# A two-layer decoder on one core: kinds of TensorE products in the plan, a planned expert stage, the last routing group in parts, and one PSUM bank for sums and output

## The chip, the cores and the metric

The kernel runs on one core of a Trainium2 chip. The metric is the device time of one execution in microseconds; lower is better. Engines are named as in the profile: PE (TensorE matmul), PEld (its weight loads), DVE (VectorE), ACT (ScalarE), POOL (GpSimd) and SP (SyncE, whose queue issues most transfers).

## The reference

The input is x of 16 sequences by 256 tokens by 256 features, in float32, with a context of 77 tokens per sequence. Six steps follow one another, each of the form x = x + f(layernorm(x)):

```python
x = x + _L0_attn_ref(_layernorm(x), ...)    # causal linear attention, 16 heads of 16
x = x + _L0_xattn_ref(_layernorm(x), ctx, mask, ...)  # softmax cross attention, 16 heads of 16
x = x + _L0_ffn_ref(_layernorm(x), gate_w, w1, w2)    # 16 experts, top 2, capacity 640 rows
x = x + _L1_attn_ref(_layernorm(x), ...)    # softmax attention, 8 heads of 64, low-rank keys and values
x = x + _L1_xattn_ref(_layernorm(x), ctx, ctx, ..., mask)  # one head of 256
x = x + _L1_ffn_ref(_layernorm(x), ...)     # gated FFN, weights and activations rounded to grids
```

In the expert step every token picks its two best experts by a sigmoid of gate products. A token's row number in its expert's batch is its rank, counted over all tokens in order; ranks of 640 and more are dropped:

```python
logits = xf @ gate_w.T; probs = sigmoid(logits); top_vals, sel = top_k(probs, 2)
weights = top_vals / (top_vals.sum(-1) + 1e-6)
ranks = cumsum(onehot(sel))[sel] - 1; valid = ranks < 640
padded[sel * 640 + ranks] = xf            # scatter
h = gelu(padded @ w1[e]); y = h @ w2[e]   # per expert
out = sum over the two of weights * y[slot]   # gather
```

So no expert can start before the last token has been routed.

## The kernel before, in words

The 4096 tokens are 32 tiles of 128 (NT = 32), four tiles to a group (NG = 8); x stays in SBUF. All products are in float32. The stages follow one another: `l0_attention`, `l0_cross` (which also routes tokens and ends with `latent_weights` and `cross_weights`, products that merge layer 1's weight matrices), `l0_experts`, `l1_tokens` (gathers the experts' rows, then both attentions of layer 1) and `l1_ffn`.

**The plan.** Three of the stages (`l0_attention`, `l0_cross`, `l1_tokens`) record their operations in a `Plan` and issue them afterwards in an order worked out from estimated times. A recorded operation is a `Call`, or several TensorE calls under `together()` which use separate parts of the array side by side. In `Plan.issue` every engine looks at the operations whose inputs are ready, finds the earliest possible begin, and takes the lowest rank among those that can begin within `near` = 150 ns of it. The rank is the place in program order, moved by `urgent`. Before, TensorE pays 100 ns in the plan when it passes from a single product to a group or back:

```python
parts = len(op.calls) > 1
busy += 100 if parts != split else 0
```

A transfer on SP is planned as 60 ns of issue and 2500 ns to landing. `Ring` keeps count of a pool's buffers: a tile can start when the tile that had its buffer before is done, and tiles with one tag start in the order in which they were made. Everything planned shows line L322 in the profile, so instructions are told apart by the tiles they write and read.

**Normalisation.** `layernorm` and `layernorm_act` take statistics on DVE (`bn_stats`, `bn_aggr`), add 1e-5 on DVE (`ln_var`, `la_var`: 128 x 4 values for four tiles), raise to the power -0.5 on POOL (`ln_rstd`, `la_rstd`), and scale on DVE or ACT (`h`, `rh`).

**Cross attention.** For each tile `scores(i)` makes products in two row halves of the array (`ps_sc`), adds the mask (`lx_s`, DVE), takes maxima (`lx_mx`, DVE), subtracts (POOL), exponentiates (ACT) and sums (`lx_sum`, DVE). `weighted(i)` transposes the weights (`ps_pt`, copied to `lx_sT`), spreads and transposes the reciprocals of the sums (`ps_rec`, copied to `rT`), multiplies by the values in column parts (`ps_av`), scales (`lx_aT`), multiplies by the output matrix into the free half of `ps_rec`, and adds to x. The eight PSUM banks are: two for the ring `pp`, four for `ps_sc`, two for the ring `pm` in which `ps_rec` and `ps_av` alternate. `l0_attention` has the same layout and a similar `weighted(i)`.

**Routing.** `R.take(g)` is a generator whose steps are mixed into the tiles of the next group: normalisation (`rh`), transposes (`ps_rt`, `rhT`), gate products (`ps_logit`), the two best experts (`rt_top`, `rt_sel`), counts (`rt_hits`, `rt_cum` on POOL), ranks by products with a triangular matrix (`ps_rank`), row numbers (`slot`), and then eight indirect transfers from POOL's queue, which scatter the rows to `moe_x` in DRAM. The last group is routed after the last tile:

```python
        step(route, 8)
        step(R.take(NG - 1), 8)
```

**Experts.** `l0_experts` is not planned; the compiler's scheduler orders it. For each of the 16 experts SP loads `w1`, `w2` (the tile `w`, 512 KB each) and the 640 rows `ex_xg`, whose load waits for every scatter; PE transposes the rows (`ps_xT`), multiplies by w1 (`ps_h`, Gelu on ACT) and by w2 (`ps_y`), DVE copies to `ex_y`, and SP stores the 640 rows to `moe_y`. Between experts, `ffn_weights` rounds the three weight matrices of the last FFN to their grid (`fw_w`, `fw_s` on DVE) and transposes them (`ps_wT`): 12 transposes for each matrix.

## Time and profile before

| | us |
|---|---|
| median of three runs | 1785.4 |
| lowest and highest of them | 1784.87, 1789.61 |
| the profiled execution, its time | 1783.88 |
| the profiled execution, its span (first to last instruction) | 1782.1 |
| busy in the span: PE, DVE, ACT, POOL | 1634.5, 1131.0, 697.9, 502.9 |
| last x of `l0_attention` | 278.5 |
| last x of `l0_cross` (tile 31) | 609.9 |
| first `ps_h` of the experts | 661.8 |
| last store of the experts issued | 966.4 |

The profile shows one execution. A group row of it reads: line, engine, operation, tile written and tiles read, shape, count, then busy time, mean duration of one in ns, and the idle time of the engine just before these instructions with what ended it. A timeline row reads: start, duration, engine, line, operation, tiles, count, and in brackets idle time before it with its releaser. Matmuls are pipelined and their ends are modelled, so the distance from one start to the next says more of PE than the duration. A float32 product appears as two matmul records.

### The profile page before, as it was taken

To read this page: it belongs to the slowest core of one execution; us is meant where nothing else is said; L and a number is where in the kernel's file an instruction comes from. 1 tells how busy PE (TensorE), PEld (TensorE's weight loads), DVE (VectorE), ACT (ScalarE), POOL (GpSimd) and SP (SyncE) were. 2 spreads that over 40 slices of the span, in tenths; PEclk is the share of its full clock that TensorE was granted. 3 is DMA by queue.
4 is the path that set the end of the run, shared out by engine and by line. 5 is a ranking of instruction groups with operands and counts; after the bars stand their busy time and mean duration, and the time that the engine had idled before them with its cause. 6 is when DMAs were issued, how large, how long until landed. Compare 5 with 4: busy or idle time off the path is not lost.

```text
span 1782.1 us, 24580 instructions
## 1 busy us (share of the span) xinstructions
PE 1634.5 (92%) x9428; PEld 1077.5 (60%) x9428; DVE 1131.0 (63%) x2290; ACT 697.9 (39%) x1467; POOL 502.9 (28%) x547
## 2 busy tenths in 40 slices
PE   5999997999999769999997799999999599989899
PEld 3666664666666557777776466666666344434388
DVE  7867667998888633221212789876767543998751
ACT  2223222655555311111111455465556233656650
POOL 6333213455556420000001776534334100000000
PEclk9999998999999769999999899999999699999999
DMA  5000007210111133343341111000000000000011
GB/s 174 1 1 1 1 1 241 66 32 28 34 34 37 57 131 118 108 147 119 107 133 50 51 57 36 28 1 1 1 1 1 1 0 0 1 0 0 0 45 50
DMA packets 73375, 84.48 MB, mean 47 GB/s; under 512 B 11614, under 2 KB 64566, under 8 KB 73258
## 3 DMA queue, kind: packets, MB, share of 16 engines
q1 hardware_dynamic: 67114, 66.35, 11.7%
q0 software_dynamic: 6144, 16.57, 2.9%
q8 instruction: 74, 1.21, 0.3%
q14 instruction: 43, 0.35, 0.1%
HBM read 49.56 MB, written 33.56 MB: 47 GB/s over the span
## 4 chain that ended last, share of the span: by engine, by line
PE 66%; DVE 21%; issue 7%; ACT 3%; POOL 2%; DMA 1%; SPq 0%; POOLq 0%; DVEq 0%; ACTq 0%
PE ps_h L422 8%; PE ps_y L422 8%; PE ps_pr L322 7%; PE ps_av L322 7%; PE ps_sc L322 6%; PE ps_gate L422 5%; PE ps_out L422 5%; PE ps_pt L322 4%; PE ps_v L322 3%; PE ps_rec L322 3%; PE ps_po L322 3%; DVE x L322 2%; DVE ff_g L1794 2%; DVE ff_ps L1681 2%; PE ps_ht L322 1%
## 5 line engine op out<-in xcount | busy, mean ns | idle before, releaser
L1558 DVE COPY ex_y<-ps_y 128x256 f32<-128x256 f32 x80 | 34.0, 424 | 231.3 <-PE ps_y L422 231.3
L422 PE MATMUL ps_up<-ff_x,ffn_up 128*128 128x512 f32 x384 | 167.6, 595 | 10.6 <-DVE ff_pu L1681 7.8
L322 POOL DMA_INDIRECT ex_yg<-moe_y,slot x64 | 63.2, 988 | 341.6 <-DMA moe_y<-ex_y 321.2
L322 POOL TENSOR_TENSOR sa_e<-sa_e,sa_rec 128x1024 f32<-128x1024 f32 x64 | 121.4, 1904 | 118.0 <-PE ps_pt L322 62.7
L322 ACT ACTIVATE sa_e<-ps_sc,sa_top 128x256 f32<-128x256 f32 x256 | 118.4, 485 | 69.1 <-DVE sa_top L322 65.0
L422 PE MATMUL ps_h<-ex_xT,w 128*128 128x320 f32 x512 | 142.8, 437 | 0.0
L422 PE MATMUL ps_y<-w,ex_h 128*128 128x256 f32 x640 | 140.7, 379 | 0.0
L422 PEld LDWEIGHTS ps_up<-ff_x,ffn_up 128*128 128x128 f32 x384 | 72.1, 190 | 105.9 <-issue 83.0
L422 PEld LDWEIGHTS ps_y<-w,ex_h 128*128 128x128 f32 x640 | 121.6, 190 | 18.2
L1548 ACT ACTIVATE ex_h<-ps_h 128x640 f32<-128x640 f32 x64 | 45.1, 704 | 221.3 <-PE ps_h L422 221.3
L422 PEld LDWEIGHTS ps_h<-ex_xT,w 128*128 128x128 f32 x512 | 96.7, 191 | 40.0 <-issue 0.6
L322 POOL TENSOR_TENSOR lx_s<-lx_s,lx_mx 128x616 f32<-128x616 f32 x64 | 77.5, 1224 | 51.6 <-DVE lx_mx L322 35.1
L422 PE MATMUL ps_out<-ffn_down,ff_g 128*128 128x256 f32 x384 | 85.3, 386 | 7.3 <-issue 7.3
L422 PE MATMUL ps_gate<-ff_x,ffn_gate 128*128 128x512 f32 x192 | 85.4, 608 | 6.4 <-DVE ff_x L1773 6.4
L422 PEld LDWEIGHTS ps_out<-ffn_down,ff_g 128*128 128x128 f32 x384 | 74.4, 194 | 18.7 <-issue 8.1
L322 ACT COPY lx_sT<-ps_pt 77x512 f32<-77x512 f32 x117 | 65.4, 581 | 49.8 <-PE ps_pt L322 49.4
L322 DVE TENSOR_TENSOR la_at<-ps_sc,la_tri 128x1024 f32<-128x1024 f32 x64 | 76.0, 1217 | 13.9 <-PE ps_sc L322 13.9
L322 PE MATMUL ps_pt<-ident,lx_s 128*77 128x128 f32 x512 | 77.0, 285 | 6.4 <-DVE rt_hits L322 3.7
L322 DVE TENSOR_REDUCE sa_top<-ps_sc 128x4 f32<-128x1024 f32 x64 | 75.9, 1214 | 10.7 <-PE ps_sc L322 10.7
L322 PE MATMUL ps_ht<-ident,h 128*128 128x128 f32 x256 | 38.8, 293 | 42.1 <-DVE h L322 24.8
L322 PEld LDWEIGHTS ps_pt<-ident,lx_s 128*77 128x77 f32 x512 | 58.7, 150 | 25.4 <-issue 10.7
L322 POOL DMA_INDIRECT moe_x<-rh,slot x64 | 63.5, 992 | 27.7 <-issue 10.1
(295 smaller groups left out, 3419.4 us busy)
## 6 DMA issues: line engine op xcount, KB each, us to landing
w<-in_L_ffn_w SPq DMA_DIRECT2D x32, 512.0 KB, 4.4
moe_x<-rt_zero SPq DMA_DIRECT2D x16, 640.0 KB, 7.6
ex_xg<-moe_x SPq DMA_DIRECT2D x16, 640.0 KB, 6.9
moe_y<-ex_y SPq DMA_DIRECT2D x16, 640.0 KB, 5.9
x<-in_x SPq DMA_DIRECT2D x32, 128.0 KB, 3.2
out_x<-x SPq DMA_DIRECT2D x32, 128.0 KB, 1.7
w_ctx_T<-in_ctx_T SPq DMA_DIRECT2D x1, 1232.0 KB
lx_bias<-in_mask_Bx1xSxS_ff SPq DMA_DIRECT2D x8, 154.0 KB, 2.4
```

The costliest lines, as they stand in the source:

```text
L322: made = getattr(getattr(self.nc, self.engine), self.method)(*self.args, **self.kwargs)
L422: E.nc.tensor.matmul(ps, a, b, start=n == 0, stop=n == last)
L1548: nc.scalar.activation(h[:, f, :].rearrange("p (a c) -> p a c", a=2), ps[:, :, :HC], AF.Gelu)
L1558: nc.vector.tensor_copy(y[:, c, :], ps)
L1681: E.nc.vector.tensor_reduce(out, in_, axis, ALU.max, apply_absolute_value=True)
L1794: nc.vector.scalar_tensor_tensor(gp, low16(gq, I16), sg16, low16(sig, U16), ALU.mult, ALU.mult)
```

## The change

Six things change.

1. `Plan` knows three kinds of TensorE operation: "all" (a single product), "row" (a `together` group whose parts use up to 64 rows and all columns) and "col" (the other groups). A table `CHANGE` gives the ns between two operations by their kinds; it enters the begin time when TensorE's next operation is chosen. The busy time of a group adds its parts by kind.
2. The normalisations' add of 1e-5 is done on POOL, just before the power, with a constant tile `E.eps`.
3. In both attentions of layer 0, the reciprocals, the sums and the output product of a tile share one bank, `ps_rec`; the sums stand in its first half, and the copy `rT` is made after the sums. In `l0_cross` ring `pp` gets three banks and `pm` one, and the sums of both halves of the heads are one `together` group; in `l1_tokens` both halves of the keys are one group.
4. `R.take` takes a first tile and a number of tiles. The last group is routed in three parts: tiles 28 and 29, tile 30, tile 31, each begun when its last tile has been computed. A scatter's rank is moved back by `later` = 300 operations, for the last two parts by 0. The steps of the last part come after the last tile.
5. `l0_experts` is planned, with rings for its pools. The first expert's rows are loaded in five pieces of 128 rows; the last expert's rows are stored in five.
6. `ffn_weights` records into the same plan, with a PSUM bank of its own.

```diff
+    CHANGE = {
+        ("all", "all"): 0, ("all", "row"): 95, ("all", "col"): 95,
+        ("row", "all"): 205, ("row", "row"): 107, ("row", "col"): 205,
+        ("col", "all"): 120, ("col", "row"): 115, ("col", "col"): 25,
+    }
...
                     begin = max(start, free[call.engine])
+                    if call.engine == "tensor":
+                        begin = max(start, free["tensor"] + self.CHANGE[last, op.first])
...
-                parts = len(op.calls) > 1
-                busy += 100 if parts != split else 0
-                split = parts
+                last = op.last
...
-        parts = {}
+        time, kind, parts = 0, op.first, {}
         for c in op.calls:
+            if c.kind != kind:
+                time += max(parts.values()) + self.CHANGE[kind, c.kind]
+                kind, parts = c.kind, {}
             parts[c.part] = parts.get(c.part, 0) + c.busy
-        return max(parts.values())
+        return time + max(parts.values())
...
+            if together:
+                self.kind = "row" if left.ap[0][1] <= 64 and out.ap[0][1] == P else "col"
...
-    var = pool.tile([P, 4], F32, name="ln_var", tag="ln_var")
-    nc.vector.tensor_scalar(var[:, :n], mv[:, :n, 1], 1e-5, None, ALU.add)
     rstd = pool.tile([P, 4], F32, name="ln_rstd", tag="ln_rstd")
-    nc.gpsimd.tensor_tensor(rstd[:, :n], var[:, :n], E.neghalf[:, :n], ALU.pow)
+    nc.gpsimd.tensor_tensor(rstd[:, :n], mv[:, :n, 1], E.eps[:, :n], ALU.add)
+    nc.gpsimd.tensor_tensor(rstd[:, :n], rstd[:, :n], E.neghalf[:, :n], ALU.pow)
...
-    def take(g):
+    def take(i0, n=4, later=300):
...
             for k in range(2):
-                nc.gpsimd.indirect_dma_start(
+                with nc.urgent(-later):
+                    nc.gpsimd.indirect_dma_start(
...
-        pp = nc.ring(ctx.enter_context(tc.tile_pool(name="lx_pp", bufs=2, space=PSUM)), 2)
+        pp = nc.ring(ctx.enter_context(tc.tile_pool(name="lx_pp", bufs=3, space=PSUM)), 3)
...
-        pm = nc.ring(ctx.enter_context(tc.tile_pool(name="lx_pm", bufs=2, space=PSUM)), 2)
+        pm = nc.ring(ctx.enter_context(tc.tile_pool(name="lx_pm", bufs=1, space=PSUM)), 1)
...
-                    pr[:, m * P : (m + 1) * P],
+                    pr[:, D + m * P : D + (m + 1) * P],
...
-            rT = w3.tile([P, D], F32, name="lx_rT", tag="lx_rT", bufs=2)
-            nc.copy(rT, pr[:, :D])
-            av = pm.tile([P, 512], F32, name="ps_av", tag="pm")
-            for m in range(KD):
-                with nc.together():
+            with nc.together():
+                for m in range(KD):
                     for par in range(2):
                         for j in range(4):
                             nc.tensor.matmul(
-                                av[32 * j : 32 * j + 32, m * P : (m + 1) * P],
+                                pr[32 * j : 32 * j + 32, m * P : (m + 1) * P],
...
+            rT = w3.tile([P, D], F32, name="lx_rT", tag="lx_rT", bufs=2)
+            nc.copy(rT, pr[:, D:])
             aT = w3.tile([P, D], F32, name="lx_aT", tag="lx_aT", bufs=2)
-            nc.vector.tensor_tensor(aT, av[:, :D], rT, ALU.mult)
+            nc.vector.tensor_tensor(aT, pr[:, :D], rT, ALU.mult)
...
-                route = R.take(g - 1) if g else none
+                route = R.take(4 * g - 4) if g else none
...
-            step(route)
+            step(route, 1 if g < NG - 1 else 3)
...
             step(mine)
-        step(route, 8)
-        step(R.take(NG - 1), 8)
+            if g == NG - 1 and a:
+
+                with nc.urgent(-80):
+                    step(route, 8)
+                    step(last, 8)
+                    last = R.take(i - 1, 2) if a == 1 else R.take(i, 1, 0)
+                    step(last, 3)
+        step(last, 8)
...
-    with ExitStack() as ctx:
-        wk = ctx.enter_context(tc.tile_pool(name="ex_w", bufs=2))
...
+    with ExitStack() as ctx, planned(E) as nc:
+        wm = nc.ring(ctx.enter_context(tc.tile_pool(name="ex_m", bufs=2)), 2)
+        wk = nc.ring(ctx.enter_context(tc.tile_pool(name="ex_w", bufs=2)), 2)
...
+            for c in range(0, CT, CT if e else 1):
+                cs = slice(c, c + (CT if e else 1))
+                nc.sync.dma_start(xg[:, cs, :], rows[:, cs, :], then=behind_scatters)
...
-            between(e)
+            rows = routed.yd[batch, :].rearrange("(c p) d -> p c d", p=P)
+            n = 1 if e == NE - 1 else CT
+            for c in range(0, CT, n):
+                nc.sync.dma_start(rows[:, c : c + n, :], y[:, c : c + n, :])
+            between(e, pw)
...
     def make(name, psum, tag):
+        nc = E.nc
+        wk = made.setdefault("ring", nc.ring(pool, 2)) if not made else made["ring"]
```

## The prediction

> **What bounds the kernel now.** I read the busy times by stage first, then the chain of waits, then the timeline where the chain is not TensorE. The first view has columns for length, busy time (instructions) of PE, PE's weight loads, DVE, ACT and POOL, granted clock, DMA share and GB/s.
>
> ```profile
> core 0: us, PE busy (x) PEld busy (x) DVE busy (x) ACT busy (x) POOL busy (x), PEclk, DMA share, GB/s
> 46.00:275.00 229.00, 225.00 (x2170) 151.41 (x2172) 158.53 (x291) 64.32 (x140) 64.48 (x92) 1.00 0.01 1
> 307.00:552.00 245.00, 223.80 (x1886) 149.46 (x1887) 219.84 (x532) 131.77 (x250) 128.43 (x153) 0.95 0.14 45
> 552.00:610.00 58.00, 51.46 (x463) 36.49 (x461) 44.79 (x124) 26.93 (x50) 31.59 (x41) 0.88 0.09 30
> 610.00:662.00 52.00, 30.15 (x127) 23.66 (x128) 22.54 (x56) 8.24 (x16) 14.00 (x16) 0.59 0.35 120
> 662.00:966.50 304.50, 303.11 (x1316) 235.73 (x1314) 66.77 (x165) 47.59 (x69) 0.00 (x0) 1.00 0.35 114
> 1000.00:1417.00 417.00, 395.61 (x2202) 258.66 (x2198) 315.97 (x671) 220.71 (x745) 198.11 (x145) 0.97 0.05 15
> ```
>
> Rows 1, 5 and 6 (first attention, experts, layer 1) have PE busy 98%, 99.5% and 95%: there only less PE work helps. Row 2 (cross attention with routing) has PE at 91% and DVE at 90%, neither full. In row 4 the kernel is between two stages: 52 us, PE busy 30 of it, at 0.59 of its clock. So the places to gain in are rows 2 to 4. A group row and the timeline say what slows row 2:
>
> ```profile
> L322 DVE TENSOR_SCALAR la_var<-la_mv 128x4 f32<-128x4 f32 x7 | 14.9, 2132 | 0.2
> 577.69 2.46 DVE L322 TENSOR_SCALAR la_var<-la_mv 128x4 f32<-128x4 f32 x1
> 577.70 2.41 POOL L322 TENSOR_TENSOR lx_s<-lx_s,lx_mx 128x616 f32<-128x616 f32 x2
> 580.23 1.04 POOL L322 TENSOR_TENSOR la_rstd<-la_var,neghalf 128x4 f32<-128x4 f32 x1
> 580.53 1.13 PE L322 MATMUL ps_rec<-w_L_xattn_wo,lx_aT 128*128 128x256 f32 x4 [2.69 <-DVE lx_aT L322]
> ```
>
> A DVE instruction on 4 columns takes 2132 ns on average, and in the example 2.46 us, exactly as long as the two POOL subtractions beside it (577.70, 2.41 us for two); at 610.57, with POOL on a scatter, it took 0.17. DVE held behind POOL makes lx_aT late, and PE idles 2.69 us. The chain of waits has this instruction at 2.63, 1.82, 2.60, 2.57, 2.58 and 2.47 us, at 376.68 to 577.69, once per group of four tiles. Now the hand-over between cross attention and experts:
>
> ```profile
> 609.44 0.42 DVE L322 TENSOR_TENSOR x<-x,ps_rec 128x256 f32<-128x256 f32 x1 [1.22 <-PE ps_rec L322]
> 617.13 3.60 PE L322 MATMUL ps_logit<-w_L_ffn_gate_wT,rhT 128*128 128x16 f32 x16 [0.46 <-ACT rhT L322]
> 623.95 1.74 DVE L1663 TENSOR_TENSOR fw_w<-fw_w,fw_r 128x1536 f32<-128x1536 f32 x1
> 631.48 0.66 PE L322 MATMUL ps_rank<-rt_hits,rt_before 128*128 128x64 f32 x2 [10.75 <-DVE rt_both L322]
> 646.30 0.97 POOL L322 DMA_INDIRECT moe_x<-rh,slot  x1 [0.31 <-DMA moe_x<-rh,slot]
> 648.29 0.42 DVE L322 TENSOR_TENSOR cx_vb<-ps_bv,r_L_xattn_bo 77x256 f32<-77x256 f32 x1 [1.07 <-PE ps_bv L322]
> 648.77 0.37 SPq L1519 DMA_DIRECT2D w<-in_L_ffn_w  x1
> 659.02 1.51 PE L1538 MATMUL ps_xT<-ident,ex_xg 128*128 128x128 f32 x6
> 661.82 9.75 PE L422 MATMUL ps_h<-ex_xT,w 128*128 128x320 f32 x32
> ```
>
> Tile 31 is finished at 609.86. Its group is routed only then: 16 gate products for four tiles, DVE work on FFN weights (fw_w, L1663) between the small routing instructions, PE idle 10.75 us before the ranks, the products that merge layer 1's weights (631.93 to 648.29), cx_vb, and only behind cx_vb the first expert's weights on SP (the waits of SP's queue give L1519 38.3 us behind cx_vb). 52.0 us pass from tile 31 to the first ps_h.
>
> **The change part by part.** The profiled execution took 1783.9 us (span 1782.1 and 1.8 around it); the median shown is 1785.4, 1.5 more. I sum against 1783.9.
>
> *A. The normalisation's add moves from DVE to POOL.* la_var goes: six instances on the chain are 14.7 us together, and I take -14.7. ln_var goes too (40 at 276 ns, 11.0 us over the kernel), mostly where PE is the bound, so 0. POOL gets about 50 adds; the nearest row is rt_cum, 288 ns, so 14.5 us on an engine busy 28%. The add stands before the power on POOL (1.04 us) with scatters and subtractions queued behind: 0.1 us net in a handover, since a wait DVE to POOL goes. Bounds: 0 if the next DVE instruction gets stuck in the same way, -17.5 (all seven at about 2.5).
> The Trainium skill bears on this ("SBUF — State Buffer", section "SBUF: two separate sides"): DVE and POOL share a port pair, an exclusive lock which the one that starts first holds for its whole instruction. By the rule la_var would get in after one subtraction (1.2 us), and seven would be worth 8.4; the row has it waiting for two. I take the row. The rule also speaks against the change: an instruction with two SBUF inputs, such as the routing's wgt, can be caught in la_var's place, and the new POOL add takes the same pair.
>
> *B. The rest of cross attention.* The transposes' ring pp goes from two to three banks, sums and output share one (pm from two to one), scatters rank 300 operations later. The weighted sums now also stand before the copy rT[...]: a new wait on ACT (0.37 us, with lx_sT copies queued behind, for which PE's products wait). pm does not become a bottleneck through this: a tile uses it from its transposes to its x, 605.46 to 609.86 for tile 31, 4.4 us against 10.2 per tile, and before, too, ps_rec of the next tile had to wait for x of this one. For it: two scatters at 448.10 and 449.39 kept a ready subtraction back by 1.0 us. DVE is idle 25 us in row 2. I take -5 over eight groups; bounds +4 (rT) and -20 (most of that idle time).
>
> *C. Routing in the last group.* Tiles 28, 29 and 30 are now routed while 29 to 31 are computed. From the rows (statistics 0.42+0.18 a tile, max 0.16+0.09+0.17 a tile, a dozen instructions of 0.1 to 0.3) two tiles are 5.0 us of DVE and one 4.2: 9.2 us more before tile 31 is done, in row 3, where DVE is idle 13.2 of 58 us. I take +4; bounds 0 and +9.
>
> *D. From tile 31 to the first ps_h.* One tile remains: statistics 0.6, add 0.3, power 1.06, shift 0.16, one rh 0.59, two transposes 0.55, copy 0.3, gate products 3.60/4 = 0.9, exponential 0.22, DVE without fw_w between 1.5, cumulation 0.5, first rank product 0.4: 7.1, with a dozen handovers of 0.08, 8. Two scatters of tile 30 and deferred ones (0.97 and 0.30 each) stand on POOL ahead of it: +2, so 10. Then the merging products, 16.4 in the old run less the two waits for ranks and sa_aq (0.98, 0.69): 14.7, and to SP's first issue 0.5: 25. The scatters (two instead of eight) end at about 16 and are covered. Issue to first transpose stays 10.25 (648.77 to 659.02): the same 1.05 MB of weights and 0.64 MB of rows lie ahead. Rows now come in five pieces, each of which waits for all scatters, so only the last piece's transposes and copy follow, 0.8 instead of 2.8; four more issues on SP at about 0.45 delay only the loads behind (expert 1's, fw_w). Sum 36 against 52.0: -16. Bounds -22 (no queueing, pieces ahead of weights) and -9.
>
> *E. Experts in a plan.* FFN weights are no longer loaded at 609.43 but behind the loads of experts 0 and 1, and 24 transposes that ran in the gap (648.77 to 661.40) run among the experts: 24 times 0.13 = 3. Sizes and counts of ps_h and ps_y stay, 8.7 and 8.6 us an expert. The plan gives every load 2.56 us where 640 KB of rows took 6.9 to land: DVE may then stand at fw_s (1.74) with copies of ps_y behind it, and PE with its three banks. I take +3; bounds 0 and +9.
>
> *F. The last store in pieces.* The first gather waits for moe_y (issued 966.40, gather at 970.51). The last 128 KB should land in about 2.4 instead of 4.1 (x loads of 128 KB: 3.2, out_x stores: 1.7): -1.7.
>
> *G. Costs of changing kind; attention, layer 1.* The measured prices enter the plan, but it takes the lowest rank among all that can begin within 150 ns, and its prices differ by at most 98 between two choices from one state (205 against 107). So I expect nearly the same order: 0. In layer 1 the joined sums already stand together (x8 on the timeline). Attention and layer 1 have no cover where their order gets worse: ±4.
>
> Sum: -14.7 -5 +4 -16 +3 -1.7 = -30.4, so 1753.5, and 1755 on the scale of the median.
>
> **The rivals.**
> *Caught again (0.20).* The lock or PE takes over as soon as la_var is gone: A gives 3, B 0, the rest stays. -3 +4 -16 +3 -1.7 = -13.7: 1771. For it: PE is at 91% in row 2, and the skill's rule. Against: PE's 2.69 us are caused by la_var itself.
> *Cross attention was held by its waits (0.14).* With DVE's 2.5 us a group gone and a third bank, idle time closes: B gives -20, C 0. Sum -49.4: 1736. For it: row 2 loses 10% of both engines. Against: the chain there is more than half PE.
> *Slower: expert boundaries (0.06).* Compiler order has 19.0 us per expert with no gap. If the plan, with loads and copies timed too short, puts fw_w or late copies ahead of ex_xT at every boundary, PE waits for DVE 16 times; from 1.9 us each (30.4/16) the gain is gone, at 2.3 it is 1791. One fw_w instruction is 1.74, but there are only some dozen, for three weights.
>
> **How the numbers follow.** Chances 0.60 for my sum, 0.20, 0.14, 0.06. Its own range is 1746 to 1765. 1732 to 1776 takes in both faster rivals and leaves out the slow one and stacked bounds. A measurement of this kernel can tell about 0.3% (5.4 us) from no change: faster by more than that 0.92 (all of the first and third, 0.18 of the second), same 0.03, slower 0.05.
>
> **What would show it.** Right: no DVE instruction of 2.5 us on four columns, groups in cross attention of about 38 us instead of 40.7 (ps_pr of the chain at 428.79 and 469.52), at most about 38 us from tile 31 to the first ps_h with 4 gate products there, experts of 304 to 310 us, a gather about 2.5 us after the last store. Wrong: cross attention no shorter (A fell), the gap over 43 (D), PE idle at ps_xT (E), or attention or layer 1 changed by over 5 us, for which I have no mechanism.

## The result, and the profile after

The changed kernel takes 1774.2 us (median of 6 runs, 1773.2 to 1777.7) where the kernel before takes 1785.1 (6 runs): ratio 0.9941, 95% interval 0.9931 to 0.9951. It gained 10.9 us of the 30 forecast. Its profiled execution took 1773.9 us, span 1772.1. The runs fell on several chips: on some the kernel before takes about 1785 us, on others, called slower below, about 1805, and the changed kernel's ratio is 0.9941 on both kinds.

The table divides the two profiled executions into stretches; an x counts from the end of its row, everything else from the start of its row. The last column has what the prediction gave each:

| stretch | before | after | difference | predicted |
|---|---|---|---|---|
| start to the last x of `l0_attention` | 278.5 | 274.9 | -3.6 | 0 (G) |
| to x of tile 0 of cross attention | 33.9 | 36.2 | +2.3 | 0 |
| to x of tile 24 | 236.0 | 211.1 | -24.9 | -19.7 (A, B) |
| to x of tile 31 | 61.5 | 81.4 | +20.0 | +4 (C) |
| to the first `ps_h` | 52.0 | 29.7 | -22.2 | -16 (D) |
| to the last store of `moe_y` | 304.6 | 312.8 | +8.2 | +3 (E) |
| to the first gather | 4.1 | 2.6 | -1.5 | -1.7 (F) |
| to the first `ps_gate` (layer 1) | 452.4 | 462.9 | +10.5 | 0 (G) |
| to the last instruction | 359.2 | 360.5 | +1.3 | 0 |

The view of busy times by stage, with the stage limits moved to where they now lie (columns as before; planned operations now show line L337):

```profile
core 0: us, PE busy (x) PEld busy (x) DVE busy (x) ACT busy (x) POOL busy (x), PEclk, DMA share, GB/s
46.00:271.40 225.40, 222.28 (x2174) 154.98 (x2172) 158.89 (x296) 62.02 (x132) 63.71 (x95) 0.99 0.01 1
307.00:525.50 218.50, 207.22 (x1895) 147.49 (x1895) 202.24 (x518) 126.45 (x244) 128.93 (x161) 1.00 0.11 39
525.50:603.70 78.20, 60.54 (x470) 45.35 (x468) 48.74 (x160) 31.02 (x59) 40.07 (x56) 0.72 0.08 33
603.70:633.40 29.70, 17.09 (x85) 15.10 (x86) 6.33 (x30) 4.62 (x9) 5.07 (x8) 0.72 0.27 89
633.40:946.20 312.80, 306.98 (x1340) 238.55 (x1339) 79.58 (x175) 52.31 (x79) 0.00 (x0) 0.99 0.37 121
978.00:1405.80 427.80, 398.18 (x2206) 257.50 (x2204) 325.87 (x667) 211.94 (x728) 203.90 (x168) 0.98 0.05 15
```

Row 2, the ordinary groups of cross attention, has its clock at 1.00 where it was 0.95. Row 3, the last tiles, is now the longest loss: 78 us, PE busy 60.5 of them at 0.72 of its clock. Row 4, the hand-over, has shrunk from 52 to 30. Of the stalls in the group rows, DVE's `la_var` is gone, and the add on POOL takes 204 ns, less than the 288 of the row that the prediction took for it:

```profile
L337 POOL TENSOR_TENSOR la_rstd<-la_mv,eps 128x4 f32<-128x4 f32 x7 | 1.4, 204 | 0.0
L337 POOL TENSOR_TENSOR la_rstd<-la_rstd,neghalf 128x4 f32<-128x4 f32 x7 | 7.3, 1041 | 0.5
```

The timeline of the hand-over shows step D much as it was drawn up: four gate products, 21.6 us from x of tile 31 to SP's first weight load, five pieces of rows, and `fw_w` behind two experts' loads. From that first load to the first `ps_xT` it is 6.0 us, to the first `ps_h` another 2.2:

```profile
603.19 0.42 DVE L337 TENSOR_TENSOR x<-x,ps_rec 128x256 f32<-128x256 f32 x1 [0.24 <-PE ps_rec L337]
...
608.58 1.04 PE L337 MATMUL ps_logit<-w_L_ffn_gate_wT,rhT 128*128 128x16 f32 x4
...
611.52 0.61 PE L337 MATMUL ps_rank<-rt_hits,rt_before 128*128 128x16 f32 x2 [1.90 <-DVE rt_hits L337]
...
624.71 0.42 DVE L337 TENSOR_TENSOR cx_vb<-ps_bv,r_L_xattn_bo 77x256 f32<-77x256 f32 x1 [0.37 <-PE ps_bv L337]
625.20 0.88 SPq L337 DMA_DIRECT2D w<-in_L_ffn_w  x2
626.50 2.24 SPq L337 DMA_DIRECT2D ex_xg<-moe_x  x5
...
631.00 0.67 SPq L337 DMA_DIRECT2D fw_w<-in_L_ffn_w_gate  x1
...
631.19 2.37 PE L337 MATMUL ps_xT<-ident,ex_xg 128*128 128x128 f32 x10 [6.51 <-DMA ex_xg<-moe_x]
...
633.35 1.31 PE L337 MATMUL ps_h<-ex_xT,w 128*128 128x320 f32 x2
```

The loss in the last tiles is plain in the timeline from tile 27's x to tile 28's, 22.5 us where the three tiles before it take 6 to 10 each:

```profile
545.26 0.41 DVE L337 TENSOR_TENSOR x<-x,ps_rec 128x256 f32<-128x256 f32 x1
...
550.10 2.16 PE L337 MATMUL ps_rt<-ident,rh 128*128 128x128 f32 x8 [3.87 <-ACT rh L337]
...
552.72 3.59 PE L337 MATMUL ps_logit<-w_L_ffn_gate_wT,rhT 128*128 128x16 f32 x16 [0.46 <-ACT rhT L337]
...
556.15 3.67 PE L337 MATMUL ps_pt<-ident,lx_s 128*77 128x128 f32 x16
...
567.72 0.42 DVE L337 TENSOR_TENSOR x<-x,ps_rec 128x256 f32<-128x256 f32 x1 [0.21 <-PE ps_rec L337]
```

PE waits 3.87 us for the normalised x of the group just finished, does its transposes and gate products, and only then the `ps_pt` of tile 28. The same pattern stands ahead of tiles 30 and 31, which take 17.5 and 12.2 us. A second thing is to be seen: 16 gate products took 1.85 us in an early group (at 343.60) and take 3.59 here. The windows of this stretch in steps of 3.41 us give the reason (PE busy first, the clock third from the end):

```profile
541.50:544.92 3.42, 2.39 (x18) 1.39 (x14) 3.18 (x7) 0.37 (x1) 2.52 (x4) 1.00 0.19 77
544.92:548.33 3.41, 1.13 (x7) 0.43 (x6) 2.46 (x9) 1.43 (x2) 3.14 (x5) 1.00 0.10 38
548.33:551.74 3.41, 1.65 (x7) 1.04 (x8) 1.03 (x3) 2.08 (x4) 2.90 (x4) 0.50 0.10 38
...
561.98:565.40 3.42, 3.42 (x18) 3.17 (x17) 1.93 (x8) 1.32 (x3) 0.71 (x2) 0.50 0.00 0
565.40:568.81 3.41, 3.41 (x22) 1.86 (x25) 2.14 (x5) 1.67 (x3) 2.80 (x3) 1.00 0.19 77
```

After a step with PE busy a third of the time the clock is exactly 0.50, for five steps, of which PE is busy throughout in the last three.

### The profile page after: what moved, and what is told of

Same layout as the page of the kernel before. It is cut to its first block, busy times and chain, and to the rows that moved or that the text cites. A ratio compares the mean times of both kernels' runs of the same rounds, so it can differ in the third digit from the quotient of the medians.

```text
span 1772.1 us, 24571 instructions
## 1 busy us (share of the span) xinstructions
PE 1617.4 (91%) x9436; PEld 1081.6 (61%) x9436; DVE 1123.2 (63%) x2293; ACT 689.1 (39%) x1454; POOL 511.2 (29%) x602
## 4 chain that ended last, share of the span: by engine, by line
PE 54%; DVE 27%; issue 8%; ACT 4%; DMA 3%; POOL 3%; SPq 0%; POOLq 0%; DVEq 0%; ACTq 0%
PE ps_y L337 7%; PE ps_h L337 7%; PE ps_rec L337 6%; PE ps_pr L337 5%; PE ps_out L438 5%; PE ps_gate L438 5%; PE ps_sc L337 4%; PE ps_pt L337 3%; DVE sa_top L337 2%; DVE x L337 2%; PE ps_v L337 2%; PE ps_po L337 2%; PE ps_av L337 2%; DVE lx_s L337 2%; DVE ff_g L1838 2%
## 5 line engine op out<-in xcount | busy, mean ns | idle before, releaser
L337 DVE COPY ex_y<-ps_y 128x256 f32<-128x256 f32 x80 | 33.7, 424 | 217.1 <-PE ps_y L337 217.1
L337 POOL DMA_INDIRECT ex_yg<-moe_y,slot x64 | 62.8, 982 | 349.2 <-DMA moe_y<-ex_y 330.0
L337 POOL TENSOR_TENSOR sa_e<-sa_e,sa_rec 128x1024 f32<-128x1024 f32 x64 | 121.8, 1914 | 134.0 <-PE ps_pt L337 87.8
L337 ACT ACTIVATE sa_e<-ps_sc,sa_top 128x256 f32<-128x256 f32 x256 | 117.9, 482 | 104.8 <-DVE sa_top L337 93.9
L337 PE MATMUL ps_h<-ex_xT,w 128*128 128x320 f32 x512 | 144.1, 439 | 0.5 <-ACT ex_h L337 0.5
L337 PE MATMUL ps_y<-w,ex_h 128*128 128x256 f32 x640 | 141.3, 379 | 2.7 <-DVE ex_y L337 2.7
L337 PEld LDWEIGHTS ps_y<-w,ex_h 128*128 128x128 f32 x640 | 121.4, 190 | 21.6 <-DVE ex_y L337 3.5
L337 PEld LDWEIGHTS ps_h<-ex_xT,w 128*128 128x128 f32 x512 | 96.8, 192 | 40.8 <-issue 1.4
L337 ACT ACTIVATE ex_h<-ps_h 128x640 f32<-128x640 f32 x64 | 45.0, 704 | 184.9 <-PE ps_h L337 184.9
L337 DVE TENSOR_TENSOR la_at<-ps_sc,la_tri 128x1024 f32<-128x1024 f32 x64 | 75.5, 1219 | 16.8 <-PE ps_sc L337 13.3
L337 POOL TENSOR_TENSOR lx_s<-lx_s,lx_mx 128x616 f32<-128x616 f32 x64 | 77.9, 1219 | 27.4 <-DVE lx_mx L337 18.4
L337 DVE TENSOR_REDUCE sa_top<-ps_sc 128x4 f32<-128x1024 f32 x64 | 76.1, 1215 | 14.2 <-PE ps_sc L337 14.0
L337 PE MATMUL ps_pt<-ident,lx_s 128*77 128x128 f32 x512 | 78.7, 295 | 1.4 <-DVE lx_sT L337 0.7
L337 PE MATMUL ps_ht<-ident,h 128*128 128x128 f32 x256 | 37.6, 291 | 45.8 <-DVE h L337 32.3
L337 PE MATMUL ps_pt<-ident,sa_e 128*128 128x128 f32 x512 | 65.5, 276 | 9.3 <-POOL sa_e L337 2.4
L337 POOL DMA_INDIRECT moe_x<-rh,slot x64 | 64.3, 1005 | 33.3 <-issue 11.0
L337 PEld LDWEIGHTS ps_pt<-ident,lx_s 128*77 128x77 f32 x512 | 63.9, 160 | 15.0 <-issue 5.1
```

The source lines that it names most:

```text
L337: made = getattr(getattr(self.nc, self.engine), self.method)(*self.args, **self.kwargs)
```

## The experiments

Ratios are to the kernel before on the same chip. Stretches are compared only within a kind of chip, and each comes from one profiled execution. Even there the same order of instructions can differ: in the run with the waits filled, tiles 0 to 24 of cross attention have practically the changed kernel's order on every engine, and took 216.2 us (13 of them at half clock) where the changed kernel took 211.1 (none at half clock). Three further runs with that order on chips of the faster kind took 211.2 to 212.8.

| kernel | ratio (95% interval) |
|---|---|
| changed kernel (again, on a slower chip) | 0.9941 (0.9925 to 0.9957) |
| last group routed after tile 31 | 0.9833 (0.9815 to 0.9850) |
| parts recorded behind the next tile | 0.9916 (0.9900 to 0.9933) |
| routing on its own bank | 0.9818 (0.9805 to 0.9832) |
| parts as they are, waits filled | 0.9927 (0.9911 to 0.9943) |
| layer 1's sums apart | 0.9954 (0.9938 to 0.9971) |
| add on DVE | 0.9957 (0.9940 to 0.9974) |
| old prices | 0.9862 (0.9842 to 0.9882) |
| price left out of the choice | 0.9977 (0.9968 to 0.9985) |
| experts not planned | 0.9929 (0.9911 to 0.9946) |
| before, with the add on POOL | 0.9942 (0.9925 to 0.9958) |
| old prices, last group routed after | 0.9752 (0.9740 to 0.9765) |
| last group routed after; old prices and add on DVE in layer 1 alone | 0.9808 (0.9795 to 0.9820) |
| own bank and old prices | 0.9749 (0.9735 to 0.9763) |
| the same, `ex_y` by either engine | 0.9734 (0.9721 to 0.9748) |

### Why the last tiles got slower (step C)

My theory was the ring. In the plan, `slot_time` lets a tile of ring `pp` start only when the tile made before it has started; the routing's `ps_rt`, `ps_logit` and `ps_rank` are in that ring together with `ps_pt`. In the last group `step(route, 3)` and `step(last, 3)` make them ahead of the next tile's `ps_pt`. The rival was the routing's own work or its place in the order. One correction to the expectations below: they speak of the routing's urgency, but `urgent(-80)` moves the rank back. The routing was meant to give way there; the ring does not let it.

Routed after, as before the change:

```diff
-            step(route, 1 if g < NG - 1 else 3)      # both places
+            step(route)
-            if g == NG - 1 and a: ...                # the parts
-        step(last, 8)
+        step(route, 8)
+        step(R.take(4 * NG - 4), 8)
```

> The changed kernel with the last group routed as before: all four tiles after tile 31, group 6 in single steps. From x of tile 24 to x of tile 31 the kernel before took 61.5 us, the changed one 81.4. If the routing in parts is what holds the last tiles (theory), that stretch falls to 60 to 66 us, and the stretch from tile 31 to the first ps_h grows from 29.8 to 40 to 48, because four tiles are routed there again: about 1768 us in all, slightly faster than the changed kernel. If instead the single bank pm or the plan's new prices slow the last tiles (rival), the stretch stays above 75 us and the whole gets about 10 to 18 us slower than the changed kernel.

The two stretches in this run, from x of tile 24 to x of tile 31 and on to the first `ps_h`:

```profile
523.30:575.30 52.00, 45.81 (x469) 33.23 (x467) 43.34 (x123) 27.76 (x53) 31.89 (x43) 1.00 0.09 34
575.30:613.60 38.30, 20.96 (x103) 17.79 (x104) 8.76 (x39) 6.45 (x12) 11.91 (x17) 0.67 0.30 96
```

The first took 52.0 us, even less than the 61.5 of before, at full clock. The hand-over gives back only 8.6 us of that. So routing in parts cost 29.4 us and brought 8.6, and the whole came to 1754.3 us, which is the forecast by chance. The rivals named in the expectation, the single bank `pm` and the new prices, are still in place in this run, so they alone are not what held the tiles. But leaving the parts out takes away their work, too, so the ring is not yet shown. In the next run only the recorded place moves:

```diff
-            step(route, 1 if g < NG - 1 else 3)      # second place in the loop
+            step(route, 1 if g < NG - 1 else 4)
+            if g == NG - 1 and a > 1:
+                with nc.urgent(-80):
+                    step(last, 3)                    # no longer at the loop's end
```

> The changed kernel, only the place where the parts' steps are recorded is moved: the transposes and gate products of a routed part (ps_rt, ps_logit) are recorded behind the ps_pt tiles of the next tile of attention, with the same parts, work and urgency. Theory: the ring pp starts its tiles strictly in recorded order, so ps_pt of the next tile stands behind a ps_rt that needs the normalised x of the tile just done; then the stretch from x of tile 24 to x of tile 31 falls from 81.4 to about 66 us (61.5 of before and some 4 of routing work), tile 31 to the first ps_h stays at 29 to 33, and the whole is about 1760. Rival: the routing's DVE work, put ahead by its urgency, is what delays the tiles; it is the same here, so the stretch stays within 4 us of 81 and the whole within 5 us of 1774.

The stretch of 81.4 us became 67.3 and the hand-over stayed at 29.4. (The profiled execution, 1761.1 us, was the fastest of four; their median is 1768.8.) By the code a part's `ps_rank` is still recorded ahead of a later tile's `ps_pt`, and from x to x it still takes 15 us twice. And with the ring itself taken away:

```diff
-  pp = nc.ring(...(name="lx_pp", bufs=3, space=PSUM)), 3)
+  pp = nc.ring(...(name="lx_pp", bufs=2, space=PSUM)), 2)
+  rp = nc.ring(...(name="lx_rp", bufs=1, space=PSUM)), 1)
-  R = l0_router(E, W, c1, wk, w3, pp)
+  R = l0_router(E, W, c1, wk, w3, rp)
```

> The changed kernel with the routing's products (ps_rt, ps_logit, ps_rank) on a ring of their own of one bank, and pp back at two banks. Order of recording, parts and urgency stay. If the order of starting within the one ring pp is what ties ps_pt of the next tile to the routing of the last one (theory), x of tile 24 to x of tile 31 falls from 81.4 us to under 68; if the urgency of the routing alone holds the tiles, it stays above 77. From x of tile 0 to x of tile 24 the same edit shows what the third bank of pp is worth to the ordinary groups: 211 us if nothing, over 218 if it is the larger part of what step B gained.

Parts, order of recording and ranks are those of the changed kernel. The rows are the stretch from tile 24 to 31 in the changed kernel's repeat and in this run, both on the same slower chip, and in a run further below (old prices in layer 1 alone) that has the same edit and the new prices in this stage, on a chip of the faster kind:

```profile
538.15:623.63 85.48, 65.50 (x496) 48.49 (x494) 52.22 (x165) 31.56 (x61) 41.40 (x58) 0.72 0.08 30
537.15:600.02 62.87, 57.70 (x501) 43.07 (x501) 45.76 (x130) 31.83 (x62) 33.51 (x46) 0.86 0.08 30
531.02:585.88 54.86, 50.27 (x502) 37.25 (x502) 45.62 (x130) 31.49 (x62) 32.62 (x46) 1.00 0.08 30
```

So 85.5 us became 62.9, and 81.4 became 54.9, while the hand-over keeps its 29.2 (28.2 in the repeat). That is the cause: not the work, which is all there, but the ring's order. For the ordinary groups the same edit, which takes the third bank from `pp`, changed nothing on this chip (226.2 us with and without); on the faster kind they took 221.6 in the run of the third row, against 211.1 to 216.2. And even so routing in parts is not shown to be worth anything: its ratio is 0.9818 here against 0.9833 for routing after tile 31, and 0.9749 against 0.9752 with the old prices, each within the intervals.

> The changed kernel once more, as the measure for the others of this set on the same chip: about 0.994 of the kernel before, with the stretches of its first profile (cross attention from x of tile 0 to x of tile 24 211 us, to tile 31 another 81, to the first ps_h 30, layer 1 from the first gather to the first ps_gate 463).

How much of the 20 us is the clock? To see that, the changed kernel's waits were filled with products that nobody reads:

```diff
+        if i0 >= NT - 8:
+            ps = psum.tile([P, D], F32, name="ps_fill", tag="pp")
+            for _ in range(8):
+                nc.tensor.matmul(ps, E.ident, E.xs[i0 + n - 1], start=True, stop=True)
         hT = wk.tile([P, KD, 512], F32, name="rhT", tag="rhT", bufs=1)
```

> The changed kernel with work added that nobody reads: in the last four routed parts (groups 6's four tiles, 28 and 29, 30, 31), ahead of ps_rt, eight products of a normal x tile with the identity (ps_fill, some 0.45 us each), ready as soon as that x is. They stand where PE waits for rh. Theory: the waits of 2 to 5 us put PE's clock to 0.50 for 17 and 27 us (44.4 of the 81.4 us from x of tile 24 to x of tile 31); with PE busy there the clock stays at 1.00 for most of it, and the stretch falls to 62 to 72 us although PE has 14 us more to do in the whole tail; tile 31 to the first ps_h, 16.7 us of it at 0.50, falls by 2 to 5. The whole: 8 to 20 us faster than the changed kernel (0.9941). Rival: the clock is only a mark of the waits; then the stretch stays at 79 us or more, and the whole gets slower by what of the added work is not covered, up to 10 us.

The stretch took 77.2 us: between the two, and nearer to the rival. The clock over it went from 0.73 to 0.92. From tile 27 to 28, where PE's wait of 3.87 us covers the added 3.7 us, the time fell from 22.5 to 17.9 us; from 29 to 30 it fell from 17.5 to 13.9; from 30 to 31, where PE had waited only 1.75 us, it rose from 12.2 to 15.6. So the low clock made up some 8 us in the two places where the wait was long enough, as far as one profile of each can tell. How the rest of the 20 divides between the serial chain and the clock is not shown. In the whole time the gain is not clear either (0.9927 against 0.9941, within the intervals).

### Layer 1 (step G)

Three suspects: the joined sums, the add on POOL, the new prices.

```diff
-            with nc.together():
-                for kc in range(2):
+            for kc in range(2):
+                with nc.together():
```

> The changed kernel with layer 1's weighted sums (ps_av) in two joined pieces, one for each half of the keys, as before. From the first gather to the first ps_gate the kernel before took 452.4 us, the changed one 462.9. If joining all four eT is what lengthened layer 1, that stretch falls to 452 to 457 us and the whole to about 1766; if it is the new prices or the add on POOL, it stays within 3 us of 463.

Layer 1 took 465.3 us: the joined sums are not it.

Next, the add on DVE again, in `layernorm` and `layernorm_act`:

```diff
-    nc.gpsimd.tensor_tensor(rstd[:, :n], mv[:, :n, 1], E.eps[:, :n], ALU.add)
-    nc.gpsimd.tensor_tensor(rstd[:, :n], rstd[:, :n], E.neghalf[:, :n], ALU.pow)
+    nc.vector.tensor_scalar(var[:, :n], mv[:, :n, 1], 1e-5, None, ALU.add)
+    nc.gpsimd.tensor_tensor(rstd[:, :n], var[:, :n], E.neghalf[:, :n], ALU.pow)
```

> The changed kernel with the normalisations' add on DVE again (la_var and ln_var in all stages). In cross attention: if the add caught behind POOL's subtractions is still worth about 2.1 to 2.5 us a group (step A of the prediction), x of tile 24 comes 12 to 17 us later than 522.2 us; if the other edits have closed that idle time anyway, by under 5. In layer 1: if the add on POOL is what lengthened it, the stretch from the first gather to the first ps_gate falls from 462.9 to under 457; else it stays within 3 us.

Layer 1 took 458.3 us, cross attention from tile 0 to tile 24 took 221.4. For the first of these, see the next runs; for the second, the part on A. Then the old prices (this run also takes back the new reckoning of a group's busy time, which is not printed here):

```diff
-                    if call.engine == "tensor":
-                        begin = max(start, free["tensor"] + self.CHANGE[last, op.first])
-                last = op.last
+                parts = len(op.calls) > 1
+                busy += 100 if parts != split else 0
+                split = parts
```

> The changed kernel with the plan's old price for a change between kinds of products (100 ns between joined and single ones, nothing else) in all planned stages. The prediction expected no difference from the prices. If the new prices reorder layer 1 for the worse, the stretch from the first gather to the first ps_gate falls from 462.9 us to under 457, and attention, which became 3.6 us shorter (x of tile 31 at 274.9 instead of 278.5), may lose that again; if the prices do nothing, each of these stays within 2 us, and cross attention (x of tile 24 at 522.2) within 3.

Layer 1 took 458.8 us, where the changed kernel on this slower kind of chip takes 468.8: the prices cost layer 1 about 10. On a chip of the faster kind it is 455.5 against 462.9 (the run with own bank and old prices below); the other 3 us by which layer 1 is longer than before (452.4) remain open. The first attention kept its gain with the old prices (its last x at 273.1 us, on a slower chip), so that gain does not come from the prices. To see whether prices and add are two causes, both were undone in layer 1, and only the prices everywhere; both runs route the last group after tile 31 with the diff above, and the second asks `if nc.plain` (set for layer 1's plan alone) ahead of the old prices and of the add on DVE:

> The changed kernel with the last group routed after tile 31, and the plan's old price for changes of kind in all stages. Against the next one (new prices in attention and cross attention) it tells what the prices do to cross attention on one chip: x of tile 0 to x of tile 24 5 us longer than with the new prices if the first reading of the run with old prices holds, shorter by up to 11 if that reading was a difference of chips. Layer 1 at 456 to 460 by the prices alone (462.9 with new ones).

> The changed kernel with the last group routed after tile 31, and in layer 1 alone the old price and the add on DVE. If the two causes of layer 1's longer time add up (4.6 and 4.1 of 10.5 us), the stretch from the first gather to the first ps_gate is 452 to 455 us, and the whole some 9 us under the run with only the last group routed after (1754): about 1745. If they are one and the same, 458.

Layer 1 took 459.3 us with old prices and the add on POOL, 463.2 with old prices and the add on DVE. The add on DVE, which had gained 4.6 us with the new prices, loses 3.9 with the old ones. So the add is no cause of its own: such an edit reorders this stage by some 4 us either way, and only the prices stand out. In cross attention from tile 0 to 24 the first of these two runs (old prices) took 214.9 us and the second (new ones) 227.4. On slower chips four profiles with the new prices lie at 226.2 to 227.4 and two with the old ones at 214.9 and 216.5: a loss of some 10 us. On the faster kind, with the routing on its own bank, no loss is shown: 221.6 with the new prices, 219.2, 219.2 and 221.8 with the old ones.

Why do the prices harm? The prediction had put them at nothing because they differ by less than `near`. My theory was the choice itself:

```diff
+                    ready = begin
                     if call.engine == "tensor":
                         begin = max(start, free["tensor"] + self.CHANGE[last, op.first])
-                    best.setdefault(...).append((begin, op.rank, op.index, n))
+                    best.setdefault(...).append((ready, op.rank, op.index, n, begin))
...
-                    (r, i, b, n) for b, r, i, n in rows if b <= first + self.near
+                    (r, i, b, n) for t, r, i, n, b in rows if t <= first + self.near
```

> The changed kernel, but the plan leaves the price of a change of kind out where it chooses (who can begin within 150 ns of the first) and keeps it in its reckoning of time. Theory: the new prices harm because up to 205 ns is more than those 150, so that a more urgent product of another kind drops out of the choice and comes late; then layer 1 gets as short as with the old prices (from the first gather to the first ps_gate 458 to 460 us on any of the chips, where the changed kernel had 463 to 469), and cross attention gains as well. Rival: it is the reckoned times that order things badly; then layer 1 stays at 463 to 469.

Layer 1 stayed at 462.8 us, and the whole got slower (0.9977): the theory falls, and the rival of the reckoned times is left. Of these, the new reckoning inside groups is not it: a run below that takes back only the price between two operations, in layer 1 alone, puts all of layer 1's instructions on PE, DVE, ACT and POOL in the same order as the old prices did, and takes the same 455.5 us. What in the price between operations misleads the plan is open. The rows are layer 1 in the changed kernel and in that run; then follow PE's waits there, in the changed kernel and in the run with own bank and old prices (total us, number of waits, longest; planned operations show L335 in runs with the old prices). They show the loss as many waits ahead of `ps_pt` and `ps_po`, not as one:

```profile
948.70:1411.60 462.90, 413.62 (x2249) 265.32 (x2247) 345.48 (x713) 217.92 (x737) 226.92 (x193) 0.96 0.07 19
925.60:1381.20 455.60, 412.64 (x2249) 267.18 (x2247) 337.39 (x704) 222.30 (x746) 226.75 (x193) 0.95 0.07 19
```

```profile
PE ps_po L337 <- ACT sa_aT L337: 5.1, 4, 2.0
...
PE ps_pt L337 <- POOL sa_e L337: 2.4, 1, 2.4
PE ps_pt L337 <- DVE hT L337: 2.3, 4, 1.4
PE ps_pt L337 <- ACT ff_x L337: 2.2, 2, 1.1
```

```profile
PE ps_po L335 <- ACT sa_aT L335: 3.5, 5, 0.7
...
PE ps_po L335 <- DVE sa_aT L335: 2.0, 3, 0.8
...
PE ps_pt L335 <- POOL sa_e L335: 0.7, 1, 0.7
```

### The add (step A) and the rest of cross attention (step B)

In the run with the add on DVE, cross attention loses 10.3 us of its gain against the changed kernel's profile, and 5.2 against the slowest profile with the add on POOL and the same order (216.2). So A is worth 5 to 10 us beside B (the prediction took 14.7). But not through the length of `la_var`, which with B in place is no longer caught for two subtractions:

```profile
L337 DVE TENSOR_SCALAR la_var<-la_mv 128x4 f32<-128x4 f32 (+2 forms) x9 | 4.7, 522 | 0.2
```

It took 522 ns on average, against 2132, and 995 ns at most. The one at 445.02 took 0.88 us, about as long as the one subtraction beside it still ran. A wait for `rh` behind it (2.12 us at 450.58) was followed by a clock of 0.50, as were two more such waits in this run: 0.97 over the stretch, 14 us at half. (The run with the waits filled, which has the add on POOL, also had 13 us at half clock there, so this part is not the add's alone.) And A alone on the kernel before (the diff of the add, the other way round):

> The kernel before with one edit: the normalisations' add moves to POOL. This is step A of the prediction alone: x of tile 24 comes 14.7 us earlier than 548.4 (bounds 0 and 17.5) by the rows of before, by 8.4 if POOL lets DVE in after one subtraction; if la_var was caught only because DVE had time, by under 4. Layer 1 (452.4 us from the first gather to the first ps_gate) stays within 3 us if the add on POOL is not what lengthened it, and grows by 5 or more if it is. Total: 1785 less the gain.

The ratio is 0.9942 (0.9925 to 0.9958): about 10 us of 1804.5, two thirds of 14.7. That these 10 us lie in cross attention is not shown: x of tile 24 came at 553.6 us, later than the 548.4 of the kernel before, but this was a slower chip, and the kernel before was not profiled on one. Layer 1 took 453.8 us even there, so with the old prices the add on POOL does it no harm.

### The experts (step E)

The experts and FFN weights as in the kernel before (its `l0_experts` and `ffn_weights` in place of the new ones):

> The changed kernel with the experts and the FFN weights outside of a plan, in program order, as before: the row loads in one piece, the last store in one piece, the FFN weights' loads early. From the first ps_h to the last store of moe_y the kernel before took 304.6 us, the changed one 312.7. If the plan's order costs the 8.2, that stretch falls to 304 to 306, but tile 31 to the first ps_h grows from 29.8 to about 36 to 40 (loads in one piece, 24 transposes and fw_w work in the gap again) and the last store to the first gather from 2.6 to 4.1: about 1774 again. If the 24 transposes alone cost it, the gap grows by as much as the experts lose, and only step F's 1.5 us is lost.

The experts took 304.6 us, but the hand-over grew to 38.3 and the store to the gather to 4.1. Against the changed kernel on the same kind of chip (313.2, 28.2, 2.6) the experts' plan, with the loads and stores that belong to it, loses 8.6 us and wins 10.1 and 1.5: by these stretches a gain of 3.0, not a loss of 8. In the whole time neither is seen (0.9929 without the plan, 0.9941 with it, within the intervals). PE's waits in the experts, changed kernel first, then this run:

```profile
PE ps_y L337 <- DVE ex_y L337: 2.7, 2, 2.3
PE ps_xT L337 <- DVE ex_y L337: 1.0, 1, 1.0
```

```profile
PE ps_k L337 <- DVE ex_y L1588: 0.5, 1, 0.5
```

The first two are waits for copies behind the FFN weights' DVE work, 3.7 us. By the rows of the experts before and after, PE is busy 3.9 us more (24 transposes more) and idle 4.4 us more, which makes up the 8.2. The remedy for the copies was tried on top of own bank and old prices together (the two diffs above):

> The changed kernel with two of the earlier edits at once: the routing's products on a bank of their own (pp at two banks), and the plan's old price for changes of kind. If the gains of the two add up (0.9941 to 0.9818 for the bank, 0.9941 to 0.9862 for the prices), the ratio to the kernel before is 0.972 to 0.976, the fastest so far; if both cure the same waits in cross attention, 0.980.

> As the run with the bank of its own and the old prices, and in the experts the copies of ps_y to ex_y go to DVE or ACT, whichever is free by the plan. If the planned experts lose time because those copies stand behind the FFN weights' DVE work (PE waited 3.7 us for ex_y), the stretch from the first ps_h to the last store falls by 3 to 5 us from 312.7; if what remains is the 24 transposes, it stays within 1 us.

The first came to 0.9749, 1740.6 us, so the two gains add up. In the second (one line: `nc.copy(y[:, c, :], ps)` in place of `nc.vector.tensor_copy`) 0.5 us of the waits for `ex_y` are left, and the experts took 311.2 us, in a repeat 307.4, against 312.6; the first of these two profiles has a wait of 2.6 us for `ex_xT` that the repeat has not. The whole gains 0.15%, within the intervals. Last, old prices in layer 1 alone, and the repeat beside it:

> As the fastest so far (bank of its own, ex_y by either engine), but the old prices in layer 1 alone; attention, cross attention and experts are planned with the new ones. Layer 1's stretch stays at 455 to 460 us, since only its own prices count there. Cross attention from x of tile 0 to x of tile 24: 211 us as in the changed kernel's first profile, so some 8 us less than the fastest so far (ratio 0.968 to 0.970) if the new prices are a gain there; 226 and a ratio of about 0.980 if the new prices are a loss there, as on the chip where the changed kernel took 1794.7 us.

> The fastest so far once more, as the measure for the other on the same chip: a ratio to the kernel before of 0.9734 within 0.002, cross attention from x of tile 0 to x of tile 24 at 215 to 222 us.

The ratios are 0.9771 (0.9757 to 0.9784) and 0.9743 (0.9730 to 0.9756): the new prices are no gain in cross attention (221.6 us with them, 219.2 without). Finally the idea of keeping PE busy was tried in the fastest version: `ps_fill` ahead of tile 31's `ps_rt` alone, and twelve such products ahead of the experts:

```diff
+        ps = pt.tile([P, D], F32, name="ps_fill", tag="pt")
+        for _ in range(12):
+            nc.tensor.matmul(ps, E.ident, E.xs[NT - 1], start=True, stop=True)
         for e in range(NE):
```

> As the fastest so far (bank of its own, old prices, ex_y by either engine), with eight such products ahead of tile 31's ps_rt, and twelve at the start of the experts, where PE waits 6 us for ex_xg. If keeping PE's clock up is worth something there, tile 31 to the first ps_h falls from 28.3 us by 1 to 4, the first expert by 1 to 2, and the ratio from 0.974 to 0.971 to 0.973; if the added products only stand in the way, both stretches get longer and the ratio is 0.975 to 0.978.

The ratio is 0.9811 (0.9798 to 0.9824): 13 us lost. The tiles 24 to 31 took 57.5 us instead of 53.8, and the hand-over 42.3 instead of 28.9. The latter is lost in one place, which DVE's timeline shows:

```profile
603.48 0.17 DVE L335 TENSOR_SCALAR slot<-rt_slot 128x2 int32<-128x2 f32 x1
...
621.31 1.75 DVE L335 TENSOR_REDUCE fw_s<-fw_w 128x48 f32<-128x1536 f32 x1 [17.66 <-DMA fw_w<-in_L_ffn_w_gate]
...
623.82 2.06 DVE L335 COPY ex_xT<-ps_xT 128x256 f32<-128x256 f32 x5
```

In the repeat without these products the `ex_xT` copies stand ahead of `fw_s` on DVE; here `fw_s` stands ahead of them, since the plan has `ps_xT` later and believes that a load lands after 2.56 us. The load of `fw_w` was issued at 612.10 and landed at about 621. DVE stood there for 17.66 us with the copies behind it, and PE waited 11.93 us. This is the mechanism of the rival "Slower: expert boundaries", at one boundary instead of sixteen. In the changed kernel `fw_s` comes right behind the first expert's copies and waits 6.2 us for its load, when no copy is due.

## Why the prediction was wrong

The direction was right and the range held the time, but the gain was a third of the forecast.

- **Step C failed; it is most of the miss.** It priced the routing's DVE instructions against DVE's idle time (+4). It did not ask in which ring the routing's products stand and what waits behind them there: with `pp` in one order, each part puts statistics, power, `rh`, transposes and gate products in series between two tiles. Measured +20.0; with the routing on a bank of its own the stretch is 54.9 us, shorter than the 61.5 of before. The clue stood in the description of the kernel before: tiles with one tag start in the order in which they were made.
- **Step G failed for layer 1.** It said that prices which differ by less than the window of 150 ns leave the order nearly as it was. Measured +10.5, the change of over 5 us for which the prediction said that it had no mechanism; the old prices give 7 to 10 us back. How the new ones misorder the stage stays open: the choice by window and the reckoning inside groups are ruled out. The prediction called the prices measured; no run here shows them.
- **Step E** was mis-sized (+3; measured +8.2). The 24 transposes were counted at 3 and PE was busy 3.9 us more; PE's waits were counted at nothing and came to 4.4 more, 3.7 of them of the kind that the step names. The part missed here was found again in D.
- **Step D** was mis-sized the other way (-16; measured -22.2, its lower bound). From x of tile 31 to SP's first issue it took 21.6 us where the sum had 25, and from there to the first `ps_xT` 6.0 where the sum kept 10.25. The rows in pieces may explain the latter; no run takes that apart. D and E together: -13 forecast, -14.0 measured; that their errors cancel was not foreseen in the sum.
- **Steps A and B**: -19.7 forecast, -24.9 measured. A is 5 to 10, not 14.7; what remains for B is 15 to 20, not 5, and which of its edits gave that is not shown. Part of it may be the clock: before, 21 of these 236 us were at half clock (0.96 over the stretch), afterwards none in the first profile. An estimate from this: with PE busy throughout, 21 us at half clock cost at most 10.5. The prediction quoted 0.95, 0.88 and 0.59 from its rows and used none of them in the sum. The row against the skill's rule ("SBUF — State Buffer", section "SBUF: two separate sides"): by the rule A was 8.4, by the row 14.7, measured 5 to 10. In the trace of before `la_var` lasted through two subtractions, with the rest of the change in place through one at most, as the rule says. The page ties the lock to DVE instructions in a 2-port mode or with two SBUF inputs; `la_var` has one input, and no run shows its mode.
- **Step F** was right (-1.5 for -1.7). Of the rivals, none came as written: cross attention up to tile 24 shortened by 24.9, between the sum's 19.7 and the fast rival's 34.7, and most of that was paid back in the last tiles.

## What to carry to other kernels

Before work is moved between the steps of a pipeline, list the buffers that it takes, and for each the order in which they are handed out: a low priority does not help work whose buffer stands ahead of others in a ring. A TensorE wait of 2 us or more can cost more than itself, since in these traces the array often ran at half its clock afterwards, for one or more steps of 3.4 us; read the clock around such waits. When a planner's costs are made more exact, measure every stage that it plans: a finer price table made one stage 7 to 10 us longer.

## What the runs showed of the hardware

**The clock.** It was 0.50 or 1.00 and changed in steps of 3.41 us. In the changed kernel it fell after a step in which PE was busy for 0.33 (at 544.92) or 0.55 (at 568.81) of the time; a step of 0.70 (at 541.50) did not bring it down. But the share of one step alone does not decide: after the first row here, 0.50, it stayed at 1.00.

```profile
312.86:316.28 3.42, 1.72 (x12) 0.77 (x10) 3.39 (x9) 1.55 (x5) 0.40 (x1) 1.00 0.00 0
568.81:572.22 3.41, 1.87 (x36) 1.37 (x34) 3.31 (x9) 1.09 (x2) 2.42 (x4) 1.00 0.18 76
```

The Trainium skill ("TensorE: Matmul & The Clock Gate", section "Part 1: The HAM clock gate (the "warmup" mystery)") gives the same two states and a free-running window of 3413 ns. Its advice ("Why this matters for your kernels") to avoid idle gaps of over about 3 us is too mild for this case, where single waits of 2.12 us (the add on DVE, at 450.58), 2.39 us (the changed kernel, at 1385.52) and 2.69 us (before, at 580.53) were followed by half clock. Others of that length were not: 2.32 us at 692.75 and 2.43 us at 989.51 of the changed kernel. The return took one step after some falls (254.8) and eight after another (27 us, from 572.23), although PE was busy throughout in two of those eight; what sets it is not shown.

**Chips.** The same kernel took 1.1% longer on some chips. In cross attention the traces show one place: in the changed kernel and its variants on such chips, between 4 and 10 of the ACT copies `lx_rT` in each profile start over 1 us after their products end; in the profiles from the other chips none does. From the repeat of the changed kernel, on a slower chip:

```profile
362.55 1.08 PE L337 MATMUL ps_rec<-lx_sT,lx_v 77*32 77x128 f32 x32
...
365.03 0.97 POOL L337 DMA_INDIRECT moe_x<-rh,slot  x1 [0.30 <-DVE lx_s L337]
366.02 0.37 ACT L337 COPY lx_rT<-ps_rec 128x256 f32<-128x256 f32 x1 [3.92 <-PE ps_pt L337]
```

Its products end at 363.63, and ACT starts 2.4 us later, as the scatter ends; the median in the changed kernel's first profile is 0.07 us. What ACT waits for is not shown and was not tried, and this is not the whole of the difference: the kernel before with the add on POOL, on a slower chip, has no such late copy.
